# Layernorm statistics of a graph layer: sent to DRAM as a column tile instead of as transposed rows

## The chip, the cores and the metric

One Trainium2 chip, one core. The metric is the device time of one execution in microseconds (us). The kernel before takes 2496.05 us, the median of 3 runs (2495.14 to 2496.59).

## What is computed

64 graphs of 256 nodes with 768 features, in fp32. `adj` is an integer adjacency matrix per graph. Cut to what matters:

```python
h = jnp.maximum(_layernorm(x, axis=-1), 0.0)          # (x - mean) / sqrt(var + 1e-5), per node
ctx = matmul(adj, h @ Wadj.T + badj) / deg            # neighbours
ctx = ctx + matmul(adj.T, h @ Wrev.T + brev) / rdeg   # reversed edges
ctx = ctx + h @ Wself.T + bself
out = x + ctx + rel                                   # rel: a few embedding rows weighted by degrees
```

## The kernel before, in words

A graph b is two tiles of 128 nodes (c = 0, 1). The three products with 768x768 weights are made by a block scheme of 15 products in fp32r, each in three passes of 4 matmuls (128x384). They run in two sweeps over the graphs: the first sweep takes eight products (in the order 10, 5, 2, 8, 11, 14, 3, 13 of the table `SWEEPS`, lines 54 to 74) for all graphs but the first and the last, which are multiplied plainly (`whole`, line 769), and stores what it has to DRAM (`keep`, line 764); the second sweep takes the other seven and the products with `adj` (`aggregate`, line 934).

A product (`product`, line 645) first prepares its left operand out of the normalised h: POOL adds blocks (`combine`, line 582, tiles named a0+a2 and the like), ScalarE (ACT) rounds them (line 600) and copies the rounded part to a PSUM tile `top` (line 607), VectorE (DVE) makes two remainders (lines 613 and 617). Then PE multiplies into a PSUM chain (x, y, z, w...; line 628), ACT rescales the chain between passes (line 666), and ACT or DVE read it out into the c tiles (lines 676, 685, 687). The next product of the same chain can't start before that read is over.

The change is in `front1` (line 699), which makes h of a graph one graph ahead. It loads x (nodes on partitions) and a transposed copy of x, `xt` (features on partitions, 6x128 elements per partition, the tile h). DVE takes the statistics of x (`bn_stats` line 713, `bn_aggr` line 717): a mean and a variance per node and tile c, four columns of a 128x128 tile `cols`, which two graphs use in turn. DVE adds epsilon (line 720) and POOL raises the variance to the power -0.5 (line 721, "pow"). h has nodes along the free dimension, so the statistics have to come as rows, the same on every partition: PE transposes `cols` (line 724), ACT copies 4 of the 128 rows out of PSUM (line 727), a DMA stores them to a DRAM tile `d` of [4, 128] (line 731), and another reads them back to all 128 partitions as the tile `row`, [128, 4, 128] (line 734). Then, for c = 0 and 1, POOL subtracts the mean ("centre", line 743) and DVE takes the maximum with 0 and multiplies by the inverse deviation ("norm", line 747), both in place on h, both with the row read again for each of the 6 feature blocks:

```python
one = lambda k, c=c: t(row)[:, 2 * c + k : 2 * c + k + 1, :].to_broadcast([P, F, P])
```

All operations are recorded with a cost and a rank (a due time plus a number from the table `OFFSETS`), and a planner (`schedule`, line 308) sets one fixed order for every engine and for SP, which issues all DMAs. On the chip each engine and SP work off their order strictly one after the other and wait with semaphores.

Of the kernel before, what the change touches and what calls it, by code (L numbers as in the profile page):

```python
# [10 lines left out]
F32 = mybir.dt.float32  # L11
F32R = mybir.dt.float32r
I32 = mybir.dt.int32
AF = mybir.ActivationFunctionType
# [3 lines left out]
P = 128  # L18
# [378 lines left out]
def on_dve(n):  # L397
    return 0.155 + 0.00104 * n
# [10 lines left out]
def on_pool(n):  # L409
    return 0.18 + 0.00218 * n  # L410
# [6 lines left out]
def on_queue(kb):  # L417
    return kb / 330.0


def record(nc, plan, fixed, B, NREL, part=None):
    F, C, H = 6, 2, 768
    NBASE = NREL // 2
    v = fixed
    t = lambda b: b.tile
# [16 lines left out]
    def dve(took, rank, name, reads, writes, emit, lock=False):  # L442
        plan.op("DVE", took, rank, name, reads, writes, emit, lock)

    def act(took, rank, name, reads, writes, emit):
        plan.op("ACT", took, rank, name, reads, writes, emit)

    def pool(took, rank, name, reads, writes, emit):
        plan.op("POOL", took, rank, name, reads, writes, emit, True)

    def pe(took, rank, name, reads, writes, emit):
        plan.op("PE", took, rank, name, reads, writes, emit)

    def dma(kb, rank, name, reads, writes, emit):
        plan.op("SP", on_queue(kb), rank, name, reads, writes, emit)

    raws, words = {}, {}
    hold = plan.buf("Q", [P, 2, 512], F32, "hold") if part != 2 else None
    if part is not None:
        one = plan.buf(None, None, None, "any")  # L460
# [238 lines left out]
    def front1(b):  # L699
        r = start1[b]  # L700
        xs = [plan.buf("BA"[c and b in regular], [P, H], F32, f"x{c}_{b}") for c in range(C)]
        hs = hT[b] = [plan.buf("B", [P, F, P], F32, f"h{c}_{b}") for c in range(C)]
        stats = plan.buf("S", [P, C, 2, 6], F32, f"stats_{b}")
        col = v["cols"][b % 2]
        for c in range(C):
            dma(384, r - 28.0 + c, f"x{c} {b}", [], [xs[c]], lambda c=c: nc.sync.dma_start(t(xs[c]), v["x"][b][:, c, :]))
        for c in range(C):
            dma(384, r - 18.0 + c, f"xt{c} {b}", [], [hT[b][c]], lambda c=c: nc.sync.dma_start(t(hs[c]), v["xt"][b, c]))
        for c in range(C):
            for n in range(2):  # L710
                dve(
                    0.55, r - 24.0 + c, f"stats {b}", [xs[c]], [(stats, (c, n))],
                    lambda c=c, n=n: nc.vector.bn_stats(t(stats)[:, c, n, :], t(xs[c])[:, ts(n, H // 2)]),
                )
            dve(
                0.21, r - 23.5 + c, f"aggr {b}", [(stats, (c, 0)), (stats, (c, 1))], [(col, c)],
                lambda c=c: nc.vector.bn_aggr(t(col)[:, 2 * c : 2 * c + 2], t(stats)[:, c, :, :]),
            )
        var = lambda: t(col)[:, :4].rearrange("p (c k) -> p c k", k=2)[:, :, 1]
        dve(0.17, r - 22.0, f"eps {b}", [col], [col], lambda: nc.vector.tensor_scalar(var(), var(), EPS, None, op0=ALU.add))  # L720
        pool(0.7, r - 21.5, f"pow {b}", [col], [col], lambda: nc.gpsimd.tensor_tensor(var(), var(), v["half"], op=ALU.pow))  # L721
        pt = plan.buf("U", None, None, f"pt_{b}", inside=hold)
        line = plan.buf("S", [P, P], F32, f"line_{b}")
        pe(0.3, r - 20.0, f"turn {b}", [col], [pt], lambda: nc.tensor.transpose(t(pt)[:, :P], t(col), v["ident"]))  # L724
        act(
            0.27, r - 19.5, f"line {b}", [pt], [line],
            lambda: nc.scalar.activation(t(line)[:4], t(pt)[:4, :P], AF.Copy),
        )
        d = plan.buf(None, None, None, "d", v["dram"].tile([4, P], F32, tag="d", name=f"d_{b}"))
        row = plan.buf("A", [P, 4, P], F32, f"row_{b}")  # L730
        dma(2, r - 19.0, f"d {b}", [line], [d], lambda: nc.sync.dma_start(t(d), t(line)[:4]))
        dma(
            400, r - 18.5, f"row {b}", [d], [row],
            lambda: nc.sync.dma_start(
                t(row).rearrange("p k i -> p (k i)"), t(d).rearrange("k p -> (k p)").partition_broadcast(P)
            ),
        )
        for c in range(C):
            h = hT[b][c]
            one = lambda k, c=c: t(row)[:, 2 * c + k : 2 * c + k + 1, :].to_broadcast([P, F, P])  # L740
            pool(
                on_pool(H), r - 12.0 + c, f"centre{c} {b}", [row, h], [h],
                lambda h=h, one=one: nc.gpsimd.tensor_tensor(t(h), t(h), one(0), op=ALU.subtract),  # L743
            )
            dve(
                on_dve(H), r - 9.0 + c, f"norm{c} {b}", [row, h], [h],
                lambda h=h, one=one: nc.vector.scalar_tensor_tensor(t(h), t(h), 0.0, one(1), op0=ALU.max, op1=ALU.mult), True,
            )
            if b not in regular:
                blocks[b, c, 1] = xs[c]  # L750
                continue
            k = kept["h", b, c] = plan.buf(None, None, None, "kept", v["kept"].tile([P, F, P], F32, name=f"kept_h{c}_{b}"))
            dma(384, r - 7.0 + c, f"keep h{c} {b}", [h], [k], lambda h=h, k=k: nc.sync.dma_start(t(k), t(h)))
        left[b] = {}
        blocks[b, 0, 1] = xs[0]
# [236 lines left out]
    if part is None:  # L992
        front1(0)
        whole(0, 0, start1[0])
        for i, n in enumerate(OPENING):
            prepare(n, 0, 20.0 + gap1 * i)
    for b in regular if part != 2 else ():
        front1(b)
        step1(b)
    if part is None:  # L1000
        front1(B - 1)
        whole(B - 1, 1, last)
        rows_prepare(last + 20.0)
        for i, n in enumerate(CHANGE):
            prepare(n, 1, last + 4.0 + gap2 * i)
    for c in range(2):
        b = v["cols"][c]
# [270 lines left out]
```

## Time and profile before

| what | value |
|---|---|
| median of 3 runs | 2496.05 us |
| the profiled execution | span 2494.7 us from first to last instruction |
| PE, DVE, ACT, POOL busy | 2467.6, 2091.7, 1787.1, 1285.3 us |
| granted TensorE clock | 1.000 over the span |
| first sweep, 104 to 1060 us | PE 955.84 of 956.00 us busy |
| bytes moved | 590.67 MB, 237 GB/s |

The profiled execution's own time is not listed apart from its span; the span is 1.35 us under the median of the runs. PE's busy share is nearly full, and a busy PE says only that matmuls were in flight: whether PE waits between them is read from the starts of its instructions, in the timeline.

### The profile page before, as it was taken

The numbers are of one execution on the slowest core, as the hardware profiler recorded it, in microseconds if no ns is written. First come the engines' busy times: TensorE is split into PE (matmuls) and PEld (weight loads), VectorE is DVE, ScalarE is ACT, GpSimd is POOL, SyncE is SP. The second block draws the span as 40 slices with busy tenths as digits, with TensorE's granted clock in tenths as the row PEclk, the third lists the DMA queues.
The fourth block names the chain that finished last, engine by engine and source line by source line (L and its number), as shares of the span: only waits on it lengthen the run. The fifth ranks groups of instructions, "written<-read, shape, count | busy, mean of one in ns | idle before, by whom it ended". The sixth has DMA issues, their size and how long they took to land.

```text
span 2494.7 us, 43472 instructions
## 1 busy us (share of the span) xinstructions
PE 2467.6 (99%) x13922; PEld 2381.1 (95%) x13922; DVE 2091.7 (84%) x3939; ACT 1787.1 (72%) x3836; POOL 1285.3 (52%) x1138
## 2 busy tenths in 40 slices
PE   7999999999999999999999999999999999999998
PEld 4899999999999999996999999999999999999998
DVE  7887787777777777778988988888888888888887
ACT  3788888888888888886666666666666666666664
POOL 1555555555555555552555555555555555555554
PEclk9999999999999999999999999999999999999999
DMA  5677777777777677776666666666666666666663
GB/s 211 235 285 266 269 281 268 268 277 271 267 282 278 260 276 282 276 274 231 209 215 216 213 212 213 213 214 213 214 214 215 215 215 216 215 215 215 213 219 130
DMA packets 224009, 590.67 MB, mean 237 GB/s; under 512 B 24056, under 2 KB 24312, under 8 KB 223776
## 3 DMA queue, kind: packets, MB, share of 16 engines
q1 hardware_dynamic: 223776, 587.86, 67.3%
q8 instruction: 110, 1.80, 0.3%
q14 instruction: 123, 1.01, 0.1%
HBM read 364.28 MB, written 223.48 MB: 236 GB/s over the span
## 4 chain that ended last, share of the span: by engine, by line
PE 96%; DMA 1%; DVE 1%; ACT 1%; issue 0%; POOL 0%; SPq 0%; DVEq 0%; ACTq 0%; POOLq 0%
PE x L628 21%; PE y L628 20%; PE agg L942 14%; PE z L628 10%; PE w L628 10%; PE t L628 5%; PE v L628 5%; PE u L628 5%; PE whole L780 2%; PE v L638 1%; DMA raw<-in_Wadj_dram 0%; DMA raw<-in_Wself_dram 0%; PE right L502 0%; PE pt L724 0%; DVE right L555 0%
## 5 line engine op out<-in xcount | busy, mean ns | idle before, releaser
L930 POOL TENSOR_TENSOR hl<-c,hl 128x768 fp32r<-128x768 f32 x256 | 475.3, 1857 | 649.3 <-ACT hl L926 459.2
L628 PE MATMUL x<-word,left 128*128 128x384 f32 x2976 | 592.2, 340 | 0.2 <-DVE c L687 0.2
L628 PE MATMUL y<-word,left 128*128 128x384 f32 x2976 | 573.1, 337 | 0.0
L628 PEld LDWEIGHTS x<-word,left 128*128 128x128 f32 x2976 | 517.4, 188 | 14.2 <-issue 11.0
L628 PEld LDWEIGHTS y<-word,left 128*128 128x128 f32 x2976 | 521.4, 188 | 5.3 <-ACT y L666 0.6
L942 PE MATMUL agg<-hl,a 128*128 128x384 f32 x2048 | 395.4, 335 | 0.0
L743 POOL TENSOR_TENSOR h<-h,row 128x768 f32<-128x768 f32 x128 | 235.7, 1863 | 266.5 <-DMA row<-d 217.3
L942 PEld LDWEIGHTS agg<-hl,a 128*128 128x128 f32 x2048 | 358.5, 188 | 0.5 <-issue 0.2
L628 PE MATMUL w<-word,left 128*128 128x384 f32 x1488 | 304.2, 339 | 1.4 <-DVE x L791 1.3
L628 PE MATMUL z<-word,left 128*128 128x384 f32 x1488 | 301.3, 337 | 0.2
L666 ACT ACTIVATE x<-x 128x768 f32<-128x768 f32 x248 | 191.8, 794 | 140.1 <-PE x L628 139.9
L628 PEld LDWEIGHTS z<-word,left 128*128 128x128 f32 x1488 | 260.4, 188 | 3.4 <-ACT c L676 0.4
L628 PEld LDWEIGHTS w<-word,left 128*128 128x128 f32 x1488 | 258.3, 188 | 4.5 <-DVE x L791 1.6
L953 DVE SCALAR_TENSOR_TENSOR c<-agg,rd,c 128x768 f32<-128x768 f32 x252 | 255.0, 1012 | 7.3 <-PE agg L942 4.0
L926 ACT ACTIVATE hl<-c 128x768 fp32r<-128x768 f32 x256 | 215.1, 841 | 32.1 <-DVE c L685 24.3
L666 ACT ACTIVATE y<-y 128x768 f32<-128x768 f32 x248 | 197.3, 796 | 44.4 <-PE y L628 44.4
L617 DVE SCALAR_TENSOR_TENSOR left<-left,top 128x256 fp32r<-128x256 f32 x496 | 199.2, 412 | 6.3
L617 DVE SCALAR_TENSOR_TENSOR left<-left 128x256 fp32r<-128x256 f32 x434 | 203.0, 489 | 0.1
L685 DVE TENSOR_TENSOR c<-c,v 128x768 f32<-128x768 f32 x124 | 117.3, 946 | 101.5 <-PE v L628 100.5
L607 ACT ACTIVATE top<-left 128x256 f32<-128x256 f32 x496 | 181.2, 383 | 6.6 <-DVE left L617 2.6
L721 POOL TENSOR_TENSOR cols<-cols,half 128x2 f32<-128x2 f32 x64 | 83.9, 1311 | 152.9 <-DVE cols L720 152.9
L676 ACT ACTIVATE c<-y 128x768 f32<-128x768 f32 x124 | 100.9, 814 | 71.7 <-PE y L628 71.7
(138 smaller groups left out, 4343.8 us busy)
## 6 DMA issues: line engine op xcount, KB each, us to landing
c<-kept SPq DMA_DIRECT2D x316, 384.0 KB
kept<-c SPq DMA_DIRECT2D x252, 384.0 KB
x<-in_x_dram SPq DMA_DIRECT2D x128, 384.0 KB
h<-in_x_t_dram SPq DMA_DIRECT2D x128, 384.0 KB
out_dram<-c SPq DMA_DIRECT2D x126, 384.0 KB
kept_h<-h SPq DMA_DIRECT2D x124, 384.0 KB
h<-kept_h SPq DMA_DIRECT2D x124, 384.0 KB
adj<-in_adj_dram SPq DMA_DIRECT2D x64, 512.0 KB
```

The costliest lines, as they stand in the source:

```text
L607: lambda: nc.scalar.activation(view(top), t(w)[:, 0].bitcast(F32), AF.Copy),
L617: lambda: nc.vector.scalar_tensor_tensor(t(w)[:, 2], t(w)[:, 1].bitcast(F32), -STEP, first(), op0=ALU.mult, op1=ALU.add), s == 1,
L628: nc.tensor.matmul(t(q)[:, half, : H // 2], t(w)[:, lw, f, :], t(r[rw])[:, f, ts(half, H // 2)], start=start and i == 0 and f == 0, stop=s ...
L666: lambda: nc.scalar.activation(view(), view(), AF.Copy, scale=scale),
L676: lambda o=o, sign=sign: nc.scalar.activation(t(o).rearrange("p (k n) -> p k n", k=2), view(), AF.Copy, scale=sign * (1.0 if value_last el ...
L685: emit = lambda to=to, op=op: nc.vector.tensor_tensor(to(), to(), view(), op=op)
L721: pool(0.7, r - 21.5, f"pow {b}", [col], [col], lambda: nc.gpsimd.tensor_tensor(var(), var(), v["half"], op=ALU.pow))
L743: lambda h=h, one=one: nc.gpsimd.tensor_tensor(t(h), t(h), one(0), op=ALU.subtract),
L926: lambda: nc.scalar.activation(t(pair)[:, 0], t(o), AF.Copy, scale=LOWER),
L930: lambda: nc.gpsimd.tensor_tensor(t(pair)[:, 1], t(o), t(pair)[:, 0].bitcast(F32), op=ALU.subtract),
L942: nc.tensor.matmul(t(q)[:, half, : H // 2], t(s["a"])[:, c, k, ts(ic, P)], t(pairs[c])[:, part, ts(half, H // 2)], start=(c == 0 and part ...
L953: lambda q=q, to=to, ic=ic: nc.vector.scalar_tensor_tensor(to(), t(q)[:, :, : H // 2], t(rd)[:, ic, k : k + 1], to(), op0=ALU.mult, op1=AL ...
```

## The change

The statistics go into a small tile of their own, [128, 4], one per graph (called line in its name), instead of four columns of `cols`. PE's transpose and ACT's copy are gone. The tile is stored to DRAM as it is (`d` is now [128, 4]: 128 pieces of 16 bytes instead of 4 of 512), and read back to all partitions; `row` is now [128, 128, 4], the four statistics of a node side by side, and centre and norm read one of the four: every fourth element, a step of 16 bytes instead of 4.

```diff
-        col = v["cols"][b % 2]
+        col = plan.buf("S", [P, 2 * C], F32, f"line_{b}")
...
-        pt = plan.buf("U", None, None, f"pt_{b}", inside=hold)
-        line = plan.buf("S", [P, P], F32, f"line_{b}")
-        pe(0.3, r - 20.0, f"turn {b}", [col], [pt], lambda: nc.tensor.transpose(t(pt)[:, :P], t(col), v["ident"]))
-        act(
-            0.27, r - 19.5, f"line {b}", [pt], [line],
-            lambda: nc.scalar.activation(t(line)[:4], t(pt)[:4, :P], AF.Copy),
-        )
-        d = plan.buf(None, None, None, "d", v["dram"].tile([4, P], F32, tag="d", name=f"d_{b}"))
-        row = plan.buf("A", [P, 4, P], F32, f"row_{b}")
-        dma(2, r - 19.0, f"d {b}", [line], [d], lambda: nc.sync.dma_start(t(d), t(line)[:4]))
+        d = plan.buf(None, None, None, "d", v["dram"].tile([P, 2 * C], F32, tag="d", name=f"d_{b}"))
+        row = plan.buf("A", [P, P, 2 * C], F32, f"row_{b}")
+        dma(2, r - 19.0, f"d {b}", [col], [d], lambda: nc.sync.dma_start(t(d), t(col)))
         dma(
             400, r - 18.5, f"row {b}", [d], [row],
             lambda: nc.sync.dma_start(
-                t(row).rearrange("p k i -> p (k i)"), t(d).rearrange("k p -> (k p)").partition_broadcast(P)
+                t(row).rearrange("p i k -> p (i k)"), t(d).rearrange("p k -> (p k)").partition_broadcast(P)
             ),
         )
...
-            one = lambda k, c=c: t(row)[:, 2 * c + k : 2 * c + k + 1, :].to_broadcast([P, F, P])
+            one = lambda k, c=c: t(row).rearrange("p i k -> p k i")[:, 2 * c + k : 2 * c + k + 1, :].to_broadcast([P, F, P])
```

Lines from 731 on have numbers lower by 7 in the changed kernel: centre is line 736 there, norm line 740, the store line 724, the row's load line 727.

The planner orders anew. On PE, before, in the first sweep (one graph; in the tile names 7 is the graph):

```order
L628 MATMUL y_7_2229<-word_2_691,left_7_2243 128x384 x4
L628 MATMUL z_7_2279<-word_1_899,left_7_2295 128x384 x4
L724 MATMUL pt_2373<-ident,cols_86 128x128
L628 MATMUL w_7_2331<-word_1_771,left_7_2182 128x384 x4
L628 MATMUL y_7_2229<-word_0_906,left_7_2342 128x384 x4
```

In the changed kernel the row of line 724 is gone and its neighbours stand as they did.

On DVE, before, around the norms (line 747) of every second graph; the last row but one is the read of chain y (product 8) that the PE row `y<-word_0_906` (product 14) waits for:

```order
L717 BN_AGGR cols_86<-stats_2719 128x2 x2
L720 TENSOR_SCALAR cols_86<-cols_86 128x2
L747 SCALAR_TENSOR_TENSOR h_10_2643<-h_10_2643,row_2651 128x768
L613 TENSOR_TENSOR left_9_2770<-a0+a1+b0+b_0_9_2699,top_9_2775 128x256
L617 SCALAR_TENSOR_TENSOR left_9_2770<-left_9_2770,top_9_2775 128x256
L747 SCALAR_TENSOR_TENSOR h_10_2655<-h_10_2655,row_2651 128x768
L687 SCALAR_TENSOR_TENSOR c_0_9_2785<-y_9_2657,c_0_9_2785 128x768
L613 TENSOR_TENSOR left_9_2768<-h_9_2441,top_9_2773 128x256
```

On DVE in the changed kernel, at the same place of the next graph:

```order
L717 BN_AGGR line_2931<-stats_2898 128x2 x2
L740 SCALAR_TENSOR_TENSOR h_11_2821<-h_11_2821,row_2829 128x768
L720 TENSOR_SCALAR line_2931<-line_2931 128x2
L740 SCALAR_TENSOR_TENSOR h_11_2833<-h_11_2833,row_2829 128x768
L613 TENSOR_TENSOR left_10_2948<-a0+a1+b0+b_0_10_2877,top_10_2954 128x256
L617 SCALAR_TENSOR_TENSOR left_10_2948<-left_10_2948,top_10_2954 128x256
L687 SCALAR_TENSOR_TENSOR c_0_10_2964<-y_10_2835,c_0_10_2964 128x768
L613 TENSOR_TENSOR left_10_2946<-h_10_2622,top_10_2952 128x256
```

This second order stood before for 30 graphs of the first sweep, the first one for the 30 in between; in the changed kernel 57 have the second. In both, the two norms come ahead of the read of chain y.

On SP, before, the store of the statistics and what is queued behind it (`d_149` is the store):

```order
L753 DMA kept_h_6_142<-h_6_1799 128x768
L731 DMA d_149<-line_1962 4x128
L706 DMA x_8_1998<-in_x_dram 128x768
L708 DMA h_7_2001<-in_x_t_dram 128x768
L734 DMA row_2009<-d_149 128x512
L708 DMA h_7_2013<-in_x_t_dram 128x768
```

In the changed kernel these six stand in the same order; the store waits for POOL's pow instead of ACT's copy.

## Rows read from the trace of the kernel before

**Rows 1.** The page: span, and busy time of each engine.
```profile
span 2494.7 us, 43472 instructions
...
PE 2467.6 (99%) x13922; PEld 2381.1 (95%) x13922; DVE 2091.7 (84%) x3939; ACT 1787.1 (72%) x3836; POOL 1285.3 (52%) x1138
```

**Rows 2.** Stretches: length; busy us of PE, PEld, DVE, ACT, POOL; clock, DMA share, GB/s.
```profile
104.00:1060.00 956.00, 955.84 (x5485) 947.61 (x5485) 754.16 (x1637) 803.38 (x1642) 523.99 (x510) 1.00 0.74 273
```

**Rows 3.** Timeline of PE, first sweep: start, us, instruction.
```profile
510.23 0.86 PE L628 MATMUL z<-word,left 128*128 128x384 f32 x4
510.93 0.27 PE L724 MATMUL pt<-ident,cols 128*128 128x128 f32 x1
510.95 0.94 PE L628 MATMUL w<-word,left 128*128 128x384 f32 x4
511.73 1.57 PE L628 MATMUL y<-word,left 128*128 128x384 f32 x8
```

**Rows 4.** Timeline of PE, the same place of the next graph.
```profile
527.78 0.27 PE L724 MATMUL pt<-ident,cols 128*128 128x128 f32 x1
...
528.58 1.63 PE L628 MATMUL y<-word,left 128*128 128x384 f32 x8
```

**Rows 5.** Timeline of DVE, the graph of rows 3; brackets: idle before, and its releaser.
```profile
502.08 0.96 DVE L687 SCALAR_TENSOR_TENSOR c<-w,c 128x768 f32<-128x768 f32 x1 [1.09 <-ACT top L607]
...
507.04 0.91 DVE L747 SCALAR_TENSOR_TENSOR h<-h,row 128x768 f32<-128x768 f32 x1
507.86 0.17 DVE L720 TENSOR_SCALAR cols<-cols 128x2 f32<-128x2 f32 x1
507.93 0.95 DVE L747 SCALAR_TENSOR_TENSOR h<-h,row 128x768 f32<-128x768 f32 x1
508.99 0.42 DVE L613 TENSOR_TENSOR left<-a0+a1+b0+b,top 128x256 fp32r<-128x256 f32 x1
509.45 0.42 DVE L617 SCALAR_TENSOR_TENSOR left<-left,top 128x256 fp32r<-128x256 f32 x1
510.49 0.96 DVE L687 SCALAR_TENSOR_TENSOR c<-y,c 128x768 f32<-128x768 f32 x1 [0.62 <-PE y L628]
```

**Rows 6.** Timeline of DVE, the next graph.
```profile
527.53 0.95 DVE L687 SCALAR_TENSOR_TENSOR c<-y,c 128x768 f32<-128x768 f32 x1
```

**Rows 7.** Lines 743, 747, 1025 and 1027: count, ns min/median/max, first and last start.
```profile
L743 POOL TENSOR_TENSOR h<-h,row x128: 1801/1852/2557, 15.8 to 1118.5; 128x768 f32<-128x768 f32 x128
...
L747 DVE SCALAR_TENSOR_TENSOR h<-h,row x128: 905/951/2580, 17.6 to 1121.0; 128x768 f32<-128x768 f32 x128
...
L1025 DVE TENSOR_TENSOR rest<-sq,deg x1: 282/282/282, 2468.6 to 2468.6; 128x128 f32<-128x128 f32 x1
...
L1027 DVE TENSOR_REDUCE total<-rest x1: 274/274/274, 2486.0 to 2486.0; 128x1 f32<-128x128 f32 x1
```

**Rows 8.** Timeline of POOL, the graph of rows 3.
```profile
501.95 3.66 POOL L743 TENSOR_TENSOR h<-h,row 128x768 f32<-128x768 f32 x2 [3.80 <-DMA row<-d]
508.11 1.34 POOL L721 TENSOR_TENSOR cols<-cols,half 128x2 f32<-128x2 f32 x1 [2.50 <-DVE cols L720]
509.42 0.73 POOL L590 TENSOR_TENSOR b0+b<-h 128x256 f32<-128x256 f32 x1
```

**Rows 9.** Timeline of SP, the same stretch: time of issue.
```profile
512.11 0.27 SPq L731 DMA_DIRECT2D d<-line  x1
...
513.38 0.38 SPq L734 DMA_DIRECT2D row<-d  x1
```

**Rows 10.** Chain that ended last, its start: start, us, what.
```profile
6.74 0.72 POOL cols L721
8.30 3.09 DMA d<-line
11.41 4.24 DMA row<-d
15.78 1.81 POOL h L743
```

More of the change, by code (lines that the diff above doesn't have):

```diff
@@ L718, in front1 @@
             )
-        var = lambda: t(col)[:, :4].rearrange("p (c k) -> p c k", k=2)[:, :, 1]
+        var = lambda: t(col).rearrange("p (c k) -> p c k", k=2)[:, :, 1]
         dve(0.17, r - 22.0, f"eps {b}", [col], [col], lambda: nc.vector.tensor_scalar(var(), var(), EPS, None, op0=ALU.add))
         pool(0.7, r - 21.5, f"pow {b}", [col], [col], lambda: nc.gpsimd.tensor_tensor(var(), var(), v["half"], op=ALU.pow))
-        pt = plan.buf("U", None, None, f"pt_{b}", inside=hold)
-        line = plan.buf("S", [P, P], F32, f"line_{b}")
-        pe(0.3, r - 20.0, f"turn {b}", [col], [pt], lambda: nc.tensor.transpose(t(pt)[:, :P], t(col), v["ident"]))
-        act(
-            0.27, r - 19.5, f"line {b}", [pt], [line],
-            lambda: nc.scalar.activation(t(line)[:4], t(pt)[:4, :P], AF.Copy),
-        )
-        d = plan.buf(None, None, None, "d", v["dram"].tile([4, P], F32, tag="d", name=f"d_{b}"))
-        row = plan.buf("A", [P, 4, P], F32, f"row_{b}")
-        dma(2, r - 19.0, f"d {b}", [line], [d], lambda: nc.sync.dma_start(t(d), t(line)[:4]))
+        d = plan.buf(None, None, None, "d", v["dram"].tile([P, 2 * C], F32, tag="d", name=f"d_{b}"))
+        row = plan.buf("A", [P, P, 2 * C], F32, f"row_{b}")
+        dma(2, r - 19.0, f"d {b}", [col], [d], lambda: nc.sync.dma_start(t(d), t(col)))
         dma(
```

## The prediction

> **What bounds the kernel now.** I began with the page: PE is busy for 2467.6 of 2494.7 us, more than any other engine [rows 1]. That alone doesn't say that PE never waits, so I went to the stretches: in the first sweep, where the statistics are made, PE is busy for 955.84 of 956.00 us and DVE for 754.16 of them [rows 2]. Then to PE's timeline, for the distance between starts, which does show waits: four matmuls take 0.70 us (510.23 to 510.93), and a transpose with four matmuls 0.80 (510.93 to 511.73) [rows 3]. So the first sweep is PE's. Last I looked for what comes close to stopping PE near the changed code, in DVE's timeline of the same stretch. There the read of chain y, which the next product of that chain waits for, begins after 0.62 us of idle time (510.49), ends at 511.45 [rows 5], and the product starts at 511.73 [rows 3]: PE is hardly ahead of that wait. Of the second sweep the change touches nothing.
>
> **What is removed.** 64 transposes. Each costs PE 0.80 - 0.70 = 0.10 us [rows 3], not the 0.27 that its row shows, since it overlaps its neighbours: 64 x 0.10 = 6.4 us, on the path. In every second graph the read of y comes later by DVE's order, right behind the second norm: it ends at 528.48 [rows 6], the product starts at 528.58 and its first eight matmuls take 1.63 instead of 1.57 us [rows 3, 4], a wait of 0.06. The new order of DVE has all graphs but a few as in rows 5, so 30 x 0.06 = 1.8 us go too. ACT's 64 copies count for nothing: ACT is busy for 803.38 us of the 956.00 [rows 2], and its own work follows PE.
>
> In the opening the chain of waits runs through the statistics of the first graph: pow ends at 7.46 and the store is issued at 8.30 [rows 10]. Without transpose and copy 0.84 us go there.
>
> **What is added: the reads at a step of 16 bytes.** No row of before shows such a read. For norm the ends are 0.95 us, as now (nothing for the step), and 2.58, the longest norm in the trace [rows 7]. For the lower end speaks a DVE operation on 128 elements that reads `deg` at a step of 8 bytes: 282 ns, beside 274 for one that reads 128 in a row [rows 7]; but 8 bytes isn't 16. I take a mechanism in between, two turns of the read for each element: from 282 ns at 128 elements and 951 at 768 one element takes 669 / 640 = 1.05 ns and the rest 0.15 us; with two turns 0.15 + 768 x 2.09 ns = **1.76 us**. That is midway between the ends (1.77), and nearest to it stands POOL's operation on the very same operands, 1.85 us.
>
> [...]
>
> Now what 2 x 0.81 = 1.62 us of norm per graph do. In the new order both norms stand ahead of the read of y on DVE. Rows 5 show no other gap of note from 502.08 on than the 0.62 us before the read: statistics, norms and remainders run back to back. So the read is later by 1.62 - 0.62 = 1.00. The next product can take little of that: from rows 3 and 5 it starts 0.28 us behind the read's end, where in rows 4 and 6 the same distance is 0.10 with 0.06 more of a wait after it, so 0.16 is needed, 0.12 is spare, and removing the transpose between uses 0.10 of it. PE then waits 1.00 - 0.02 = **0.98 us in each graph**. The wait doesn't die out: DVE's stretch starts at 502.08 on a release by ACT [rows 5], which follows PE, so in the next graph all is late together and the norms are again too long. Behind the waiting read stand the remainders for the following products; behind the waiting matmuls stands all of PE. 60 graphs have the norms in such a place (57 of the new order and 3 much like it): 60 x 0.98 = 59 us.
>
> For centre the ends are 1.85 and 2.56, the longest [rows 7]; I take 2.2. Nothing on the path in the steady stretch: the two end at 505.61 [rows 8], would end at 506.3, at the worst at 507.1, and the second norm starts at 507.93 [rows 5]. That cover is gone when one centre takes over 2.99 (507.93 - 501.95, halved). Pow ends 0.57 us behind the second norm [rows 5, 8]; if it goes on doing so it is 1.6 later, at about 511.05, and POOL's b0+b1 behind it too; the left operand that needs b0+b1 first is wanted by PE only in the next graph's products.
>
> In the opening one centre and one norm are on the chain: 0.35 + 0.81 = 1.2 us more.
>
> **The DMAs.** SP stands at the store until ACT's copy is over, issues it at 512.11, and the row's load at 513.38 [rows 9], so a store lands within 1.27 us there; in the opening it took 3.09 [rows 10]. The new store is 128 pieces of 16 bytes instead of 4 of 512. Its bounds: nothing, and the opening's duration, 1.8 us later. It can be issued when pow is over, at about 511.05 with long norms, 1.0 us earlier, and the loads of x and xt behind it move with it. So the row comes between 1.0 earlier and 0.8 later; centre has 2.3 us before the second norm (505.61 to 507.93) and needs 0.7 of it. I count nothing, and take the worse end into the range.
>
> **The sum**, against the profiled execution: span 2494.7 - 6.4 - 1.8 - 0.8 + 59 + 1.2 = 2545.9. The median of the runs stands 1.35 above that span, so **2547 us**, 2.0% slower.
>
> **Rivals.** What a measurement of this kernel can tell from no change is about 0.2%, 5 us.
>
> *Norm keeps its pace.* If a step of 16 bytes costs DVE nothing, the removals remain: 2496 - 6.4 - 1.8 - 0.8 = 2487, faster by 0.36%. For it: the step of 8 bytes is free, and reading no more than one element for each result leaves no reason in the rows for a second turn. Against it: three of four elements are skipped now, not one of two. The mechanism decides at one point: the waits eat the gain where 60 x (2 x d - 0.62 - 0.02) = 8.2, that is where norm gets d = 0.39 us longer, 1.34 us. [...] Chance 0.36.
>
> *The gain and the wait cancel.* Norm at 1.28 to 1.42 us: within 5 us of 2496. A narrow window; 0.09.
>
> *The small store is late.* If it lands some 4 us after its issue, SP holds the row and the loads behind it, centre starts after 503, and the norms wait for centre: each us beyond that is another us per graph, 60 us in all. Against it: 3.09 us in the opening, behind large loads. On top of short norms 2550; 0.04.
>
> *Norm at its worst*, 2.58 us: 60 x (3.26 - 0.64) = 157 us, 2645. 0.03.
>
> That the change isn't what it says I leave out: in the new order of PE the transposes are gone and the rest stands.
>
> **How the numbers follow.** The forecast, norm between 1.45 and 1.87 us, has 0.48; its own range is 2510 (60 x 0.36 = 22 us of waits, less 8) to 2562 (60 x 1.20 = 72, less 8, and 2 for the opening). Faster by over 0.2%: 0.36. Within 0.2%: 0.09. Slower: 0.48 + 0.04 + 0.03 = 0.55. The range for 8 in 10 has to take in the first rival, so it goes from 2485 to 2562; it leaves out the worst norm and most of the late store.
>
> **What would show it.** Right: norm (line 740) near 1.76 us, the read of y (line 687) without idle time before it, PE waiting about 1 us per graph before the y product for DVE's c, 17.7 us per graph instead of 16.85 (from one transpose to the next, 510.93 to 527.78). Wrong: norm at 0.95 us and the idle time before the read still 0.62; then PE's stretches of the first sweep are full and 0.10 to 0.16 us per graph are gone. POOL waiting for the row longer than now would speak for the late store.

## The result, and the profile after

The changed kernel takes **2524.07 us**, the median of 4 runs (2521.3 to 2524.87), beside 2495.89 us for the kernel before (4 runs, 2495.14 to 2496.59). The ratio is 1.0111, with a 95% interval of 1.0097 to 1.0125. It is slower, as forecast, and inside the range, but by 28 us where the sum said 51.

The page, to be read beside [rows 1]:

```profile
span 2522.1 us, 43218 instructions
...
PE 2485.3 (99%) x13858; PEld 2387.0 (95%) x13858; DVE 2162.4 (86%) x3939; ACT 1783.1 (71%) x3772; POOL 1372.8 (54%) x1138
```

64 matmuls and 64 ScalarE operations are gone, and DVE has 70.7 and POOL 87.5 us more to do. PE is "busy" 17.7 us longer with 64 instructions less. That is no work: matmuls that are spread out by a wait stay counted as busy (below, eight of them show 1.69 us around a wait, and 1.57 without one).

The stretch of the first sweep (length; busy us of PE, PEld, DVE, ACT, POOL; clock, DMA share, GB/s), beside [rows 2]:

```profile
104.00:1060.00 956.00, 950.91 (x5342) 932.16 (x5341) 802.65 (x1633) 786.29 (x1561) 593.82 (x504) 1.00 0.80 269
```

(PEld is the loading of weights into PE.) PE now has 5.09 us of plain idle time where it had 0.16, and 143 matmuls fewer were begun in the same 956 us, of which only some 57 are the transposes. The clock is the same, 1.00.

The two operations that read the row, by line (count, ns min/median/max, first and last start), beside [rows 7]:

```profile
L740 DVE SCALAR_TENSOR_TENSOR h<-h,row x128: 1496/1542/2795, 18.3 to 1134.8; 128x768 f32<-128x768 f32 x128
...
L736 POOL TENSOR_TENSOR h<-h,row x128: 2185/2250/2897, 16.1 to 1130.5; 128x768 f32<-128x768 f32 x128
```

Norm went from 951 to 1542 ns, centre from 1852 to 2250. The next view is DVE's timeline in the graph that answers to [rows 5] (start, us, instruction; idle time would stand in brackets):

```profile
498.43 1.50 DVE L740 SCALAR_TENSOR_TENSOR h<-h,row 128x768 f32<-128x768 f32 x1
499.85 0.16 DVE L720 TENSOR_SCALAR line<-line 128x2 f32<-128x2 f32 x1
499.92 1.55 DVE L740 SCALAR_TENSOR_TENSOR h<-h,row 128x768 f32<-128x768 f32 x1
501.38 0.41 DVE L613 TENSOR_TENSOR left<-a0+a1+b0+b,top 128x256 fp32r<-128x256 f32 x1
501.83 0.42 DVE L617 SCALAR_TENSOR_TENSOR left<-left,top 128x256 fp32r<-128x256 f32 x1
502.17 0.95 DVE L687 SCALAR_TENSOR_TENSOR c<-y,c 128x768 f32<-128x768 f32 x1
```

The bracket before the read of y (line 687) is gone: the 0.62 us of idle time are used up, and the read ends at 503.12. PE's timeline of the same place, beside [rows 3]:

```profile
500.23 1.57 PE L628 MATMUL y<-word,left 128*128 128x384 f32 x8
501.64 0.86 PE L628 MATMUL z<-word,left 128*128 128x384 f32 x4
502.33 0.87 PE L628 MATMUL w<-word,left 128*128 128x384 f32 x4
503.17 1.69 PE L628 MATMUL y<-word,left 128*128 128x384 f32 x8
```

Four matmuls without a wait take 0.70 us from start to start [rows 3]. From 502.33 to 503.17 it is 0.84, and the eight that follow show 1.69 us instead of 1.57: a stall of about 0.26 us, right behind the read's end. The view of waits puts a sum to it (engine, line, who is waited for: us, times, longest), 104 to 1060 us:

```profile
PEld y L628 <- DVE c L687: 19.9, 55, 1.0
```

and of before:

```profile
PEld y L628 <- DVE c L687: 0.3, 1, 0.3
```

19.9 us, where the kernel before has 0.3. (PE itself shows 3.4 us of this wait, 7 times; these stand at the same moments as 7 of the 55 and add nothing.) This is the mechanism of the forecast, in its place, at a third of its price of 59 us.

To see where the rest of the 28 us lies, I cut each profiled execution at the read of y in the first sweep and at an ACT copy that every graph has in the second. The rows by line (count, ns min/median/max, first and last start), first of before:

```profile
L687 DVE SCALAR_TENSOR_TENSOR c<-y,c x62: 948/956/958, 89.5 to 1122.9; 128x768 f32<-128x768 f32 x62
...
L917 ACT ACTIVATE token<-pt x64: 277/277/279, 1157.3 to 2471.4; 128x128 fp32r<-128x128 f32 x64
```

and of after:

```profile
L687 DVE SCALAR_TENSOR_TENSOR c<-y,c x62: 948/949/958, 90.4 to 1140.9; 128x768 f32<-128x768 f32 x62
...
L910 ACT ACTIVATE token<-pt x64: 277/278/283, 1177.6 to 2499.8; 128x128 fp32r<-128x128 f32 x64
```

| stretch | before | after | difference |
|---|---|---|---|
| start to the first read of y | 89.5 | 90.4 | +0.9 |
| first sweep (61 graphs on) | 1033.4 | 1050.5 | **+17.1** |
| between the sweeps | 34.4 | 36.7 | +2.3 |
| second sweep (63 graphs on) | 1314.1 | 1322.2 | **+8.1** |
| to the end | 23.3 | 22.3 | -1.0 |
| span | 2494.7 | 2522.1 | +27.4 |

The second sweep, of which the prediction said that the change touches nothing, is 8 us longer. That was the surprise to explain.

Last, the store. SP's timeline (time of issue), beside [rows 9]:

```profile
502.06 0.32 SPq L724 DMA_DIRECT2D d<-line  x1
...
505.02 0.33 SPq L727 DMA_DIRECT2D row<-d  x1
```

and the opening's chain, beside [rows 10]:

```profile
7.32 4.01 DMA d<-line
11.35 4.61 DMA row<-d
16.10 2.19 POOL h L736
```

The row's load follows 2.96 us behind the store's issue, not 1.27. In the opening the store goes out 0.98 us earlier, lands 0.92 us slower, and the row is issued at 11.35 instead of 11.41: nothing was gained.

### The profile page after: what moved, and what is told of

Read it like the earlier page. It is cut to its first block, busy times and chain, and to the rows that moved or that the text cites. A ratio compares the mean times of both kernels' runs of the same rounds, so it can differ in the third digit from the quotient of the medians.

```text
span 2522.1 us, 43218 instructions
## 1 busy us (share of the span) xinstructions
PE 2485.3 (99%) x13858; PEld 2387.0 (95%) x13858; DVE 2162.4 (86%) x3939; ACT 1783.1 (71%) x3772; POOL 1372.8 (54%) x1138
## 4 chain that ended last, share of the span: by engine, by line
PE 90%; DVE 6%; issue 2%; DMA 1%; ACT 1%; POOL 0%; SPq 0%; DVEq 0%; ACTq 0%; POOLq 0%
PE x L628 21%; PE y L628 18%; PE agg L935 14%; PE w L628 9%; PE z L628 9%; PE t L628 5%; PE u L628 5%; PE v L628 5%; PE whole L773 2%; DVE h L740 1%; PE v L638 1%; DVE stats L713 1%; DVE left L613 1%; DVE c L687 1%; DVE left L617 1%
## 5 line engine op out<-in xcount | busy, mean ns | idle before, releaser
L628 PE MATMUL y<-word,left 128*128 128x384 f32 x2976 | 580.0, 340 | 7.3 <-DVE c L687 4.8
L736 POOL TENSOR_TENSOR h<-h,row 128x768 f32<-128x768 f32 x128 | 286.2, 2261 | 246.5 <-DMA row<-d 191.1
L628 PEld LDWEIGHTS w<-word,left 128*128 128x128 f32 x1488 | 264.1, 188 | 1.0 <-ACT w L666 0.5
L721 POOL TENSOR_TENSOR line<-line,half 128x2 f32<-128x2 f32 x64 | 118.2, 1846 | 185.7 <-DVE line L720 179.6
L740 DVE SCALAR_TENSOR_TENSOR h<-h,row 128x768 f32<-128x768 f32 x128 | 200.7, 1576 | 7.1 <-POOL h L736 7.1
```

The source lines that it names most:

```text
L628: nc.tensor.matmul(t(q)[:, half, : H // 2], t(w)[:, lw, f, :], t(r[rw])[:, f, ts(half, H // 2)], start=start and i == 0 and f == 0, stop=s ...
```

## The experiments

Two theories stood for the slower first sweep: the norms alone, through the read of y (the prediction's), or the later row and the slower centre on POOL. For the second sweep: other places of the tiles in SBUF (the 512-byte tile `line` is gone from its class of slots, and what lies behind moves), or something that the order of the work does.

**e1_shift.** Before, with 32 unused bytes put ahead of the working tiles, to move them all together:

```diff
     half = const.tile([P, C], F32, name="half")
+    const.tile([P, 8], F32, name="shift")
```

> The kernel before, unchanged but for 32 unused bytes ahead of all its tiles in SBUF: tiles that began on a multiple of 64 bytes begin 32 off, and the reverse. Theory 1 (all of the 28 us comes from DVE's longer norms): nothing changes, 2496, 20.90 us per graph in the second sweep. Theory 2 (part of it comes from where the smaller statistics tile put all later tiles: the second sweep, whose code didn't change, went from 20.90 to 21.02 us per graph): 21.0 us per graph and about 2503 to 2510 in all.

Measured: 2495.13 us beside 2495.76, ratio 0.9999 (0.9989 to 1.0008). Moving the tiles together changes nothing that can be told (that they moved is read from the edit; no trace shows addresses).

**e2_pad.** The changed kernel with a statistics tile as wide as the one it replaced, so that its class of slots keeps its size:

```diff
-        col = plan.buf("S", [P, 2 * C], F32, f"line_{b}")
+        col = plan.buf("S", [P, P], F32, f"line_{b}")
...
-        dma(2, r - 19.0, f"d {b}", [col], [d], lambda: nc.sync.dma_start(t(d), t(col)))
+        dma(2, r - 19.0, f"d {b}", [col], [d], lambda: nc.sync.dma_start(t(d), t(col)[:, :4]))
```

> The changed kernel with the statistics tile as wide as the old line tile (128x128, four columns used), which puts the other tiles back on the addresses' grid of before; the order of all engines is that of the changed kernel. Theory 1: 2524, as changed. Theory 2: the second sweep goes back to 20.90 us per graph (7 us), the first loses some 0.1 us per graph (6 us): about 2511, with norm still at 1.54 us and PE waiting for the read of y.

Measured: 2516.46 us, ratio 1.0088 (1.0071 to 1.0105), 7.6 us under the changed kernel. The gain lies where it was lost:

```profile
L687 DVE SCALAR_TENSOR_TENSOR c<-y,c x62: 948/951/959, 89.6 to 1141.5; 128x768 f32<-128x768 f32 x62
...
L910 ACT ACTIVATE token<-pt x64: 277/278/279, 1177.8 to 2493.1; 128x128 fp32r<-128x128 f32 x64
```

These rows by line of e2 give 1315.3 us for the second sweep (1322.2 in after) and 1051.9 for the first (1050.5). The first sweep gained nothing: it is 18.5 us longer than before, where 6 were expected, and there PE waits for the read of y as in after (the row of waits is shown with e4). In the second, the matmuls with `adj` between 1300 and 2400 us show a mean of 337 ns in after and 334 in e2. These are the rows of the costliest groups (busy us, mean ns), first of after, then of e2:

```profile
L935 PE MATMUL agg<-hl,a 128*128 128x384 f32 x1680 | 328.8, 337 | 0.0
```

```profile
L935 PE MATMUL agg<-hl,a 128*128 128x384 f32 x1680 | 325.6, 334 | 0.0
```

All later variants but e8 stand on e2, so that places are out of the comparison.

**e3_unit_step.** e2 with both reads of the row at a step of one element:

```diff
-            one = lambda k, c=c: t(row).rearrange("p i k -> p k i")[:, 2 * c + k : 2 * c + k + 1, :].to_broadcast([P, F, P])
+            one = lambda k, c=c: t(row).rearrange("p (k i) s -> p k (i s)", k=4)[:, 2 * c + k : 2 * c + k + 1, :].to_broadcast([P, F, P])
```

> e2 with centre and norm reading the row at a step of one element, as before the change (they read other numbers than they should, so the output is not the reference's; operations, sizes and order are e2's). What is left of the change is the loss of the transposes and the copies and the store in 128 pieces. Theory 1: norm back at 0.95 us, no wait, 2486 to 2489, the gain that the first rival forecast. If the small store or something else costs: above 2493.

Measured: 2490.92 us, ratio 0.9981 (0.9971 to 0.9991); norm 949 ns, centre 1850. This is what the removal is worth when the reads cost nothing (the store of 128 pieces is still in it): 4.8 us, some 2 less than the least that was expected. By line:

```profile
L687 DVE SCALAR_TENSOR_TENSOR c<-y,c x62: 951/958/959, 88.2 to 1114.4; 128x768 f32<-128x768 f32 x62
```

The first sweep takes 1026.2 us, 7.2 less than before. Between the sweeps and in the second it loses some 4 us of that (36.2 instead of 34.4, and 1316.3 instead of 1314.1); why wasn't tried.

**e4_norm_only** and **e5_centre_only.** e3 with only norm, or only centre, at the step of 16 bytes:

```diff
+            flat = lambda k, c=c: t(row).rearrange("p (k i) s -> p k (i s)", k=4)[:, 2 * c + k : 2 * c + k + 1, :].to_broadcast([P, F, P])
...
-                lambda h=h, one=one: nc.gpsimd.tensor_tensor(t(h), t(h), one(0), op=ALU.subtract),
+                lambda h=h, one=flat: nc.gpsimd.tensor_tensor(t(h), t(h), one(0), op=ALU.subtract),
```

(e4; in e5 the same edit stands at norm instead.)

> e2 with only centre at a step of one element (other numbers, as in e3), norm at the step of four. Theory 1 (DVE's norm, not POOL's centre): as e2 within 3 us. The rival, that the longer centre delays norm: as e3.

> e2 with only norm at a step of one element (other numbers than it should read), centre at the step of four: 2.25 us on POOL instead of 1.85. If POOL's longer centre costs by itself, as e4 against e2 (4.8 us) may mean: about 2496. [...]

Measured: e4 2511.66 us, ratio 1.0067 (1.005 to 1.0083), norm 1540 ns; e5 2492.78 us, ratio 0.9989 (0.998 to 0.9999), centre 2252 ns. So norm alone costs 20.7 us over e3, and centre alone 1.9, which is hardly more than the intervals allow. Behind long norms centre costs more: e2 less e4 is 4.8 us. The waits from 104 to 1060 us show where, first of e4, then of e2:

```profile
PEld y L628 <- DVE c L687: 19.8, 55, 0.5
```

```profile
PEld y L628 <- DVE c L687: 23.8, 56, 1.3
```

It is the same wait before the y product, 4.0 us longer. In e2 nine norms of that stretch begin before the centre of the other tile is over on POOL, and these are drawn out, by 3.6 us in all (one takes 2.46 us, from 599.38 on, instead of 1.54; the centres end at 600.42). In e4 no norm of the stretch is. So centre's cover is not as free as the prediction had it when norm has used up DVE's slack, and the price is paid through norm.

**e10_one_norm.** Is the cost of a longer norm linear, or is it taken by gaps first? e3 with only the norm of c = 0 at the step:

```diff
-                lambda h=h, one=one: nc.vector.scalar_tensor_tensor(t(h), t(h), 0.0, one(1), op0=ALU.max, op1=ALU.mult), True,
+                lambda h=h, one=(one if c == 0 else flat): nc.vector.scalar_tensor_tensor(t(h), t(h), 0.0, one(1), op0=ALU.max, op1=ALU.mult), True,
```

> e3 with only one of the two norms (c = 0) at the step of four (other numbers, as in e3). It is 0.59 us longer per graph. Theory 1 with the gaps that e2 shows (0.62 us before the read of y and some 0.3 more between the norms and it): the gaps take it all, 2491 as e3. If the cost goes with the time added to DVE: half of what e4 lost to e3, 2501.

Measured: 2492.26 us, ratio 0.9987 (0.9978 to 0.9997). With 0.59 us more of norm in each graph it is 1.3 us over e3 (1.9 when each is taken against the kernel before in its own batch), where half of e4's loss would be 10. DVE's timeline of e10, around the read of y:

```profile
504.32 0.91 DVE L741 SCALAR_TENSOR_TENSOR h<-h,row 128x768 f32<-128x768 f32 x1
505.15 0.16 DVE L720 TENSOR_SCALAR line<-line 128x2 f32<-128x2 f32 x1
505.22 1.54 DVE L741 SCALAR_TENSOR_TENSOR h<-h,row 128x768 f32<-128x768 f32 x1
506.67 0.42 DVE L613 TENSOR_TENSOR left<-a0+a1+b0+b,top 128x256 fp32r<-128x256 f32 x1
507.12 0.42 DVE L617 SCALAR_TENSOR_TENSOR left<-left,top 128x256 fp32r<-128x256 f32 x1
507.72 0.96 DVE L687 SCALAR_TENSOR_TENSOR c<-y,c 128x768 f32<-128x768 f32 x1 [0.17 <-ACT w L666]
```

and the same three operations of e3, without any long norm:

```profile
503.81 0.95 DVE L740 SCALAR_TENSOR_TENSOR h<-h,row 128x768 f32<-128x768 f32 x1
504.85 0.42 DVE L613 TENSOR_TENSOR left<-a0+a1+b0+b,top 128x256 fp32r<-128x256 f32 x1
...
506.32 0.96 DVE L687 SCALAR_TENSOR_TENSOR c<-y,c 128x768 f32<-128x768 f32 x1 [0.59 <-ACT w L666]
```

In e3 there are two gaps: norm ends at 504.76 and the left operand starts 0.09 later; in e10 it starts 0.09 before norm's end (505.22 + 1.54 = 506.76 against 506.67). That first gap has no bracket in the view. The second falls from 0.59 to 0.17. Together 0.18 + 0.42 = 0.60: the whole of the longer norm.

**e6_step_of_two.** Could the step be 8 bytes? e2 with `d` as [2, 128, 2], stored in 256 pieces of 8 bytes, and the row to match:

```diff
-        d = plan.buf(None, None, None, "d", v["dram"].tile([P, 2 * C], F32, tag="d", name=f"d_{b}"))
-        row = plan.buf("A", [P, P, 2 * C], F32, f"row_{b}")
+        d = plan.buf(None, None, None, "d", v["dram"].tile([C, P, 2], F32, tag="d", name=f"d_{b}"))
+        row = plan.buf("A", [P, C, P, 2], F32, f"row_{b}")
...
-            one = lambda k, c=c: t(row).rearrange("p i k -> p k i")[:, 2 * c + k : 2 * c + k + 1, :].to_broadcast([P, F, P])
+            one = lambda k, c=c: t(row)[:, c].rearrange("p i k -> p k i")[:, k : k + 1, :].to_broadcast([P, F, P])
```

> e2 with the store made per tile c ([2, 128, 2] in DRAM, 256 pieces of 8 bytes), so that centre and norm read every second element, a step of 8 bytes; the output is the reference's. Theory 1 with the row of line 1025 (8 bytes cost nothing): norm 0.95 us, centre 1.85, the time of e3 plus what the smaller pieces cost: 2490 to 2493. If a step of 8 bytes costs half of what 16 cost: norm 1.25 us, no wait yet by the gaps seen in e2, 2491 to 2496.

Measured: 2505.0 us, ratio 1.0048 (1.0031 to 1.0064). Norm, centre and the store's landing, by line:

```profile
L740 DVE SCALAR_TENSOR_TENSOR h<-h,row x128: 908/950/2617, 19.4 to 1120.0; 128x768 f32<-128x768 f32 x128
...
L736 POOL TENSOR_TENSOR h<-h,row x128: 1826/1878/2574, 17.6 to 1117.3; 128x768 f32<-128x768 f32 x128
...
DMA to landing us min/median/max: 4.5/5.3/5.6
```

At the step of 8 bytes norm takes 950 ns (949 in e3) and centre 1878 (1850). But the store of 256 pieces lands 5.3 us after its issue (128 pieces in after: 3.0), and the row is late for POOL. Its waits between 104 and 1060 us:

```profile
POOL h L736 <- DMA row<-d: 254.4, 46, 7.1
```

In after that wait is 168.8 us, the longest 5.3. What a late row does stands in one graph of e6, on DVE, POOL and PE:

```profile
424.07 2.62 DVE L740 SCALAR_TENSOR_TENSOR h<-h,row 128x768 f32<-128x768 f32 x1
```

```profile
422.15 3.73 POOL L736 TENSOR_TENSOR h<-h,row 128x768 f32<-128x768 f32 x2 [7.04 <-DMA row<-d]
```

```profile
429.34 0.97 PE L628 MATMUL y<-word,left 128*128 128x384 f32 x4 [0.67 <-DVE c L687]
```

The two centres end at 425.88, 1.81 us into the norm, and that norm takes 2.62 us instead of 0.95; the read of y is late again and PE waits. Between 104 and 1060 us 33 of 113 norms run beside a centre in this way, 21.5 us longer in all. The first sweep is 12.1 us longer than that of e3 (89.9 to 1128.2). So the late store, a rival at 0.04 in the prediction, exists, by another way than was thought: in that stretch of e6 norm doesn't wait for its centre, it is drawn out by the centre of the other tile. It takes twice the pieces to make it cost this much.

**e7_step_of_one.** The same with `d` as [4, 128], 512 pieces of 4 bytes, and the row and its reads as in the kernel before:

```diff
-        d = plan.buf(None, None, None, "d", v["dram"].tile([P, 2 * C], F32, tag="d", name=f"d_{b}"))
+        d = plan.buf(None, None, None, "d", v["dram"].tile([2 * C, P], F32, tag="d", name=f"d_{b}"))
...
-        dma(2, r - 19.0, f"d {b}", [col], [d], lambda: nc.sync.dma_start(t(d), t(col)[:, :4]))
+        dma(2, r - 19.0, f"d {b}", [col], [d], lambda: nc.sync.dma_start(t(d).rearrange("k p -> p k"), t(col)[:, :4]))
```

> e2 with the store turning the tile itself ([4, 128] in DRAM, 512 pieces of 4 bytes), so that the row is as before the change, step of one; the output is the reference's. If the number of pieces matters little, as e3: 2491. The store of 128 pieces took 3.0 us to land instead of under 1.3; at 4 times as many it may take 6 to 10 us, and by the slack of about 2.3 us before the second norm that would stop PE: 2500 to 2700.

Measured: 2808.17 us, ratio 1.1248 (1.1229 to 1.1267). SP's timeline in the opening shows the price of the store:

```profile
7.20 0.37 SPq L724 DMA_DIRECT2D d<-line  x1
16.24 0.34 SPq L727 DMA_DIRECT2D row<-d  x1
```

9.0 us from the store's issue to the row's. In the steady stretch it is much the same:

```profile
514.27 0.37 SPq L724 DMA_DIRECT2D d<-line  x1
...
522.55 0.33 SPq L727 DMA_DIRECT2D row<-d  x1
```

Here it is 8.3 us; SP issues two other loads in it and stands still from 516.17 on. Over the run this wait of SP adds up to 522.2 us in 63 graphs. The first sweep takes 1339.8 us (97.9 to 1437.7): 306 us more than before, 5.0 per graph. TensorE's clock was lower there too: from 98 to 300 us PE was busy for 169.12 of 202.00 us, and the granted clock was on the mean 0.93 of full speed, where the first sweep before had 1.00. How much of the 306 us that took was not separated.

**e8_gaps.** Do relative places matter without any change of the work? Before, with the tile `line` 32 bytes wider, which nothing uses:

```diff
-        line = plan.buf("S", [P, P], F32, f"line_{b}")
+        line = plan.buf("S", [P, P + 8], F32, f"line_{b}")
```

> The kernel before, with the line tile 32 bytes wider (136 columns, 128 used): the tiles keep their order, but no longer lie all on the same place in a grid of 512 bytes, as in the changed kernel. If the places of the tiles against each other (and not where all of them begin, e1) cost the second sweep its 0.12 us per graph: 20.95 to 21.02 us there, 2500 to 2508 in all. If it was something else in the changed kernel: 2496, 20.90.

Measured: 2502.61 us, ratio 1.0028 (1.0018 to 1.0039). By line, and among the costliest groups between 1300 and 2400 us:

```profile
L917 ACT ACTIVATE token<-pt x64: 277/278/282, 1157.7 to 2477.8; 128x128 fp32r<-128x128 f32 x64
```

```profile
L942 PE MATMUL agg<-hl,a 128*128 128x384 f32 x1680 | 328.1, 337 | 0.0
```

The second sweep takes 1320.1 us (before: 1314.1), with the 337 ns of after (before: 334), and the first hardly differs (1034.7, before 1033.4). So 6 to 7 us follow from an edit that by its text only moves tiles relative to each other, with no instruction added, removed or put in another order. What of the places matters was not found.

**e9_thin_row.** Can the removal be kept and the step's price moved off DVE? e2, and POOL copies the two inverse deviations out of the row at step one, ahead of the first centre:

```diff
+                    nc.gpsimd.tensor_copy(v["thin"][0], t(row).rearrange("p i (c k) -> p k c i", k=2)[:, 1])
...
-                lambda h=h, one=one: nc.vector.scalar_tensor_tensor(t(h), t(h), 0.0, one(1), op0=ALU.max, op1=ALU.mult), True,
+                lambda h=h, inv=inv: nc.vector.scalar_tensor_tensor(t(h), t(h), 0.0, inv(), op0=ALU.max, op1=ALU.mult), True,
```

> A version made from the findings: e2, and POOL copies the two inverse deviations of the row (256 elements, step of four) once per graph into a tile of its own with a step of one, ahead of the first centre; norm reads that tile. The store stays at 128 pieces. The output is the reference's; the planner does not see the copy, so the order of all engines is that of the changed kernel. POOL has some 1.6 to 2.5 us per graph between the second centre and the first norm (e5). If that is enough for the copy (0.7 to 0.9 us): norm 0.95 us, 2491 to 2493, 0.1 to 0.2% under the kernel before. If the copy makes norm wait: above 2495.

Measured: 2493.71 us beside 2495.2, ratio 0.9996 (0.9986 to 1.0005). The copy and norm, by line:

```profile
L740 POOL COPY thin<-row x64: 623/642/660, 15.9 to 1103.6; 128x256 f32<-128x256 f32 x64
...
L749 DVE SCALAR_TENSOR_TENSOR h<-h,thin x128: 902/947/2714, 18.7 to 1110.1; 128x768 f32<-128x768 f32 x128
```

0.64 us of POOL per graph buy back 0.59 us of DVE twice, and 22.8 of e2's us. It ends level with the kernel before, just above the 2491 to 2493 that were expected. Nothing found here that computes the reference clearly beats that kernel.

## Why the prediction was right, and why by half

**Right: the place and the kind of the wait.** Norm slows by more than DVE's slack, the read of y comes late, PE waits before the y product in the graphs of the sweep. The idle time before the read is gone, PE's wait for DVE's c rose from 0.3 to 19.9 us, and taking the step from norm alone (e5 against e2) takes 23.7 us away. The first sweep takes 17.2 us per graph (1050.5 / 61; before 1033.4 / 61 = 16.9), where the sum had 17.7.

**Mis-sized: "two turns of the read for each element", 1.76 us.** Norm takes 1.542. With the 0.15 us of fixed time from the prediction, one element costs (1.542 - 0.15) / 768 = 1.81 ns instead of 1.05: 1.7 times as long, where the estimate had two turns. No run shows such turns. Both norms together are 1.18 us longer, not 1.62. By the prediction's own formula that is 1.18 - 0.62 - 0.02 = 0.54 us per graph instead of 0.98. The upper end of 2.58 us was not the price of a step either: that norm, at 1118.54 in the trace of before, runs beside a centre on POOL (1118.46 to 1120.30), as the drawn-out norms of e6 do.

**Wrong: "Rows 5 show no other gap of note from 502.08 on than the 0.62 us before the read".** There was more, in the same rows. Norm ends at 507.93 + 0.95 = 508.88, the left operand starts at 508.99 [rows 5]; in after the next operation starts 0.09 us before norm's recorded end. That is 0.20 us more. In after, where it has no idle time before it, the read starts at 502.17, 0.08 before its predecessor's recorded end (501.83 + 0.42), so the 0.62 is 0.70. Slack in this graph: 0.90. Then 1.18 - 0.90 - 0.02 = 0.26 us per graph, which is the stall seen in PE's timeline, and close to the 0.31 of e4 against e3 (1045.0 against 1026.2 us for 61 graphs). e10 shows it from the other side: 0.59 us disappear in the gaps. The point from which the mechanism decides was put at a norm of 1.34 us; with the full gaps and the gain of 8.2 us over 60 graphs it is about 0.95 + (0.14 + 0.92) / 2 = 1.48. The window of the rival in which gain and wait cancel was put too wide besides: by the prediction's own formula, within 5 us of 2496 means a norm of 1.30 to 1.38 us, not 1.28 to 1.42.

**Wrong in part: centre costs "nothing on the path in the steady stretch".** With short norms that holds (e5, 1.9 us over e3), with long ones it is 4.8 us (e2 against e4). The prediction asked only when the second norm would have to wait for centre; the runs show a norm that waits for nothing and is drawn out by a centre beside it. Centre's duration was right: 2.2 forecast, 2.250 measured. Pow is the part of that cover that went as said: it ends at 502.04, 0.57 us behind the second norm, as in [rows 5, 8]. POOL's timeline of after:

```profile
500.09 1.95 POOL L721 TENSOR_TENSOR line<-line,half 128x2 f32<-128x2 f32 x1 [3.56 <-DVE line L720]
```

**Right in the steady stretch: the removal.** 6.4 + 1.8 = 8.2 us forecast, 7.2 measured in the first sweep of e3.

**Wrong: the 0.8 us of the opening.** They were taken at their place and given back at the next: the store that goes out 0.98 us earlier needs 4.01 instead of 3.09 us. The prediction held the store's two bounds ready for the steady stretch, where the store did land 1.7 us later (2.96 against 1.27) and the first sweep of e3 still gained, and didn't set them against its own gain in the opening.

**Wrong: "Of the second sweep the change touches nothing".** No instruction there changed, but the places of the tiles did, and that is 7.6 us of the 28 (after against e2; e8 shows 7 without the change).

So the 28 us are, by the medians: -4.8 for the removal (e3), +20.7 for norm (e4 less e3), +4.8 for centre behind it (e2 less e4), +7.6 for places (after less e2). The forecast had -9.0 for the removal, +59 for norm, +1.2 for the opening and nothing for the last two. Two errors of opposite sign partly cancelled: without the places the kernel would have come out 20.7 us slower (e2), not 28. The range, 77 us wide, takes in both.

## What to carry to other kernels

A transpose that an engine does beside its work may be the cheap half of a bargain (here 4.8 us by e3, against the 20.7 of norm's reads): look at the layout that it gives to every later reader, and price the reader's step on the engine that has the least slack. Count that slack over all gaps of the engine's stretch, those of a tenth of a microsecond without a bracket too, because a longer operation can eat them one after the other before anything waits: in e10 norm is 0.59 us longer, two gaps of the graph shown give up 0.60, and the weight loads of the y product wait 0.2 us for that read from 104 to 1060 us (19.9 in after). And a change that alters a tile's size can move other tiles, which was worth 7.6 us here (after less e2): run it once with the old size as padding before a difference far from the edit is explained by the edit. Last, an operation that nothing waits for can still cost, when it runs into one on another engine and draws it out, as centre drew out nine norms of e2 by 3.6 us: look at durations as well as at waits.

## What the runs showed of the hardware

**The step of a read.** For DVE's norm (two fp32 inputs, 128x768), a step of 4 bytes takes 949 ns (e3), of 8 bytes 950 (e6), of 16 bytes 1542 (after). I had expected either no price or two turns of the read (1.76 us); the runs give the durations, and no run shows what in the read sets them.

For POOL's centre the three are 1850, 1878 and 2250 ns: 22% more at 16 bytes, where norm takes 62% more.

**Small pieces in a store to DRAM.** The same 2 KB take at most 1.27 us as 4 pieces of 512 bytes in the graph of [rows 9] (3.09 in the opening [rows 10]), 3.0 as 128 of 16 (the landing's median in after), 5.3 as 256 of 8 (the median in e6), and 8.3 and 9.0 as 512 of 4 (e7, from the store's issue to the row's, in the two places shown). In e7 SP issued nothing from 516.17 to 522.55, when the row's load went out; the load of h that is next in SP's order followed at 522.97.

**A norm beside a centre.** A norm on DVE that overlapped a centre on POOL was longer by most of the overlap: 2.62 instead of 0.95 us with 1.81 us beside a centre (e6, the norm at 424.07), 2.79 instead of 1.54 with 1.38 (after, the norm at 101.41; the centres end at 102.79).

**Places in SBUF.** A change of 32 bytes in the unused margin of one kind of tile moved the second sweep's matmuls with `adj` from 334 to 337 ns and the kernel by 0.28% (e8), while 32 bytes ahead of all the working tiles changed nothing (e1). The interval of that ratio, 1.0018 to 1.0039, doesn't take in 1, and 0.28% is more than the gain that this edit had at its best (e3, 0.19%). Its cause stays open.
